# Layer 1: the product with B in front of the last scan, the second gate projection in a done scan's bank, activation bursts in groups 2, 4 and 6; layer 0: three sums instead of four

## The chip, the cores and the metric

The kernel runs on one core of one Trainium2 chip. The metric is device time in microseconds (us). The core's engines work side by side, each with its own queue: TensorE (PE in the profile, PEld for its weight loads), VectorE (DVE), ScalarE (ACT), GpSimd (POOL) and SyncE (SP), which issues DMA transfers here.

## The reference, cut to what matters

The input is (2, 64, 256, 256) in float32. Four layers each add their result to it: x = x + layer(group_norm(x)). Layers 0 and 1 are touched by the change.

```python
# layer 0: nine shifted neighbours, each weighted by a score
feature_score = einsum('bckhw,bchw->bkhw', unfold(em), em)
comp_score = sigmoid(einsum('bckhw,c->bkhw', unfold(inp), w_comp))
out = einsum('bckhw,bkhw->bchw', unfold(inp), comp_score * feature_score)

# layer 1: two Mamba blocks, a layer norm behind each
u, res = split(x @ in_w.T)
u = silu(causal_conv(u) + conv_b)
delta = softplus((u @ xproj_w.T)[..., :r] @ dt_w.T + dt_b)
h = exp(delta * A) * h + delta * B * u        # a scan over all positions, 16 states
y = einsum('bdn,bn->bd', h, C) + u * D
y = layernorm((y * silu(res)) @ out_w.T)
```

## The kernel before

The two batches with 64 channels each fill the 128 partitions; an image row pair, or 512 positions, is the usual tile (128x512). In both layers the order of every engine's queue is the order of the program (`manual_schedule`): an instruction that waits holds up all behind it on its engine.

**Layer 0** goes through 128 steps of two rows. A step t computes the scores of step n = t - 3 on TensorE (`pf`, one matmul for the pixel itself and one for each of four neighbours A, B, C, D), multiplies with the gated features on VectorE (`mult` for the neighbour, `move` for the mirrored neighbour, which another pixel takes up), and adds the terms of step t - 4 with four identity matmuls into `acc` (lines 403 to 411). GpSimd adds the moved products into the terms C, D and B beforehand (lines 400, 401), VectorE those of A.

**Layer 1** cuts the 65536 positions into 128 chunks of 512 for each of two Mambas: 256 tasks that alternate between the first (m = 0) and the second (m = 1, three chunks behind). A task has eight groups, numbered 0 to 7: two batches b of four groups j each; a group has four scans k = 0 to 3. (g,k) below is scan k of group g. A group runs so:

- A product h = delta u B. For j = 2 GpSimd makes it ahead (`product`, line 752; it stands behind group j = 3 of the half before). For the others VectorE makes it (line 773), from B spread over the partitions by a matmul into `pb` (`spread`, line 744, one PSUM bank).
- Four scans on VectorE (line 792), each with its decay `da` from ScalarE (line 789, three PSUM banks in the pool `p_a`).
- On GpSimd the last states are copied (795) and h is multiplied with C (796).
- TensorE sums h over the states into `py` (`before`, line 802), one group later, at the fourth scan.

`gate` (line 652) multiplies a finished `py` with SiLU of the other projection, on VectorE.

Beside the scans, the task that comes two later is prepared by `front` (line 580), a generator that is moved on step by step: load and pad `xin` (`padded`, line 565, copies three columns on GpSimd; for m = 0 only, as the second Mamba's `xin` is written by the norm of the first), convolution of four taps in two halves, the projection for the gate, SiLU, the matmuls for delta and B and C, softplus, and the spill of `bc`, `delta` and `du` to DRAM. `fetch` (line 634) brings these back, laid out for the scans, in groups 1 and 5 of the task before they are used. `layer_norm` (line 656) finishes the task before, in the same way. `aside` (line 691) says in which group each step comes, always at the group's fourth scan. All matmuls of `front` and `layer_norm` take turns in three PSUM banks (`p_mm`). SiLU, softplus and logarithm need other function tables of ScalarE than the decay's exponential, so each makes a burst with a table load at both ends.

Of the kernel before, what the change touches and what calls it, by code (L numbers as in the profile page):

```python
# [10 lines left out]
F32 = mybir.dt.float32  # L11
BF16 = mybir.dt.bfloat16
AF = mybir.ActivationFunctionType
ALU = mybir.AluOpType
# [3 lines left out]
P = 128  # L18
C = 64
# [101 lines left out]
class Kernel:  # L121
# [115 lines left out]
    def layer0(self, x, y, coeffs):  # L237
# [12 lines left out]
        with ExitStack() as ctx:  # L250
# [135 lines left out]
            with tc.manual_schedule(engines={E.PE, E.DVE, E.Activation, E.Pool, E.SP}):  # L386
                features(0)
                for t in range(nstep + 5):
                    if t and t % per == 0:
                        load(t // per + 1)  # L390
                    gated = embed(t) if t < nstep else None
                    if t + 1 < nstep:
                        features(t + 1)

                    n, last = t - 3, t - 4
                    acc = None
                    if 0 <= last < nstep:
                        acc = p_o.tile([P, 2, W], F32, name="acc")
                        if last:
                            for name in "CDB":  # L400
                                add(nc.gpsimd, last, name, moved_to(last, name))

                    def out(name):
                        if acc is not None:
                            nc.tensor.matmul(
                                acc,
                                self.ident,
                                term.pop((last, name)),
                                start=name == "A",
                                stop=name == "B",  # L410
                            )

                    if 0 <= t - 2 < nstep:
                        products(t - 2)
                    if gated:
                        gated()
                    if 0 <= n < nstep:
                        g, _, j = at(n)
                        own = g[:, j : j + 2, inner]
                        pf = score(sq.pop(n))  # L420
                        part = p_s.tile([P, 2, W], F32, name="part")
                        nc.vector.tensor_tensor(part, own, pf, ALU.mult)
                        for i, name in enumerate("ABCD"):
                            pf = score(pr.pop((n, name)))
                            out("ACDB"[i])
                            mult(n, name, near(g, j, name), pf)
                            if name == "A" or n + 1 < nstep:
                                move(n, name, own, pf)
                            if name == "A":
                                nc.vector.tensor_add(part, term[n, name], part)  # L430
                                nc.vector.tensor_add(term[n, name], moved_to(n, name), part)
                    else:
                        for name in "ACDB":
                            out(name)
                    if acc is not None:
                        k, s = divmod(last, per)
                        yt = pool.tile([P, 2, W], F32, name="yt")
                        nc.vector.tensor_add(yt, xt[k][:, 2 * s : 2 * s + 2], acc)
                        nc.vector.bn_stats(stats[:, last, :], yt.rearrange("p r w -> p (r w)"))
                        nc.sync.dma_start(yv[:, 2 * last : 2 * last + 2], yt)  # L440
# [86 lines left out]
    def layer1(self, x, y, coeffs):  # L527
# [4 lines left out]
        with ExitStack() as ctx:  # L532
# [47 lines left out]
            def front(m, i, t):  # L580
# [14 lines left out]
                pr = [p_mm.tile([P, T], F32, name="mm")]  # L595
                mm(pr[0], w["res"][halves[0]], xin[halves[0], 3 : 3 + T])
                yield
                u = pool.tile([P, 2, T], F32, name="u", bufs=3)
                t["u"], t["res"] = u, []
                for b in range(2):  # L600
                    nc.scalar.activation(u[:, b], pv[b], AF.Silu, bias=w["conv_b"])
                pr.append(p_mm.tile([P, T], F32, name="mm"))
                mm(pr[1], w["res"][halves[1]], xin[halves[1], 3 : 3 + T])
                for b in range(2):
                    r = pool.tile([P, T], F32, name="res", bufs=8)
                    nc.scalar.activation(r, pr[b], AF.Silu)
# [9 lines left out]
                delta = pool.tile([P, 2, T], F32, name="delta", bufs=1)  # L616
                for b in range(2):
                    self.softplus(delta[:, b], pd[b], w["dt_b"])
                bc = pool.tile([64, T], F32, name="bc", bufs=3)
                nc.scalar.copy(bc, pb)  # L620
                du = pool.tile([P, 2, T], F32, name="du", bufs=1)
                nc.gpsimd.tensor_tensor(du, delta, u, ALU.mult)
                t["bc"] = bc

                d_bc = spill.tile([2, 32, T], F32, name="d_bc")
                nc.sync.dma_start(d_bc.rearrange("b n t -> (b n) t"), bc)
                d_dl = spill.tile([2, P, T], F32, name="d_dl")
                nc.sync.dma_start(d_dl.rearrange("b c t -> c b t"), delta)
                d_dv = spill.tile([2, P, T], F32, name="d_dv")
                nc.sync.dma_start(d_dv.rearrange("b c t -> c b t"), du)  # L630
                t["spilt"] = d_bc, d_dl, d_dv
# [24 lines left out]
            def layer_norm(m, i, t):  # L656

                po = p_mm.tile([P, T], F32, name="mm")
                for b in range(2):
                    mm(po[C * b : C * b + C], ws[m]["out"], t["res"][b])  # L660
                sq = pool.tile([P, T], F32, name="lsq", bufs=1)
                nc.scalar.activation(sq, po, AF.Square)
                if m == 1:
# [22 lines left out]
            tasks = [(m, i - 3 * m) for i in range(nch + 3) for m in range(2)]  # L686
            tasks = [(m, i) for m, i in tasks if 0 <= i < nch]
            ts = [{} for _ in tasks]
            norm = iter(())

            def aside(n):

                nonlocal norm
                t = ts[n]
                ahead = front(*tasks[n + 2], ts[n + 2]) if n + 2 < len(tasks) else iter(())

                def d(b):
                    t["py"] = p_y.tile([P, T], F32, name="py")
                    mm(t["py"], ws[tasks[n][0]]["d"], t["u"][:, b], True, False)

                def more(b):
                    if n + 1 < len(tasks):
                        fetch(ts[n + 1], b)

                next(norm, None)
                next(ahead, None)
                yield
                d(0)
                next(norm, None)
                more(0)  # L710
                next(ahead, None)
                yield
                next(ahead, None)
                yield
                next(ahead, None)
                yield
                next(ahead, None)
                yield
                d(1)
                more(1)  # L720
                next(ahead, None)
                yield
                if n:
                    norm = layer_norm(*tasks[n - 1], ts[n - 1])
                next(norm, None)
                yield
                next(norm, None)
                yield

            load(0)  # L730
            for n in range(2):
# [3 lines left out]
            with tc.manual_schedule(engines={E.PE, E.DVE, E.Activation, E.Pool, E.SP}):  # L735
# [24 lines left out]
                    )  # L760
                    return h

                ahead = {2: product(*groups[2])}
                pb, before = spread(), None
                for g, (n, b, j) in enumerate(groups):
                    if b == j == 0:
                        steps = aside(n)
                    if j == 0:
                        st = states.tile([P, 4, 4], F32, name=f"st{tasks[n][0]}{b}")
                    t, m = ts[n], tasks[n][0]  # L770
                    if j != 2:
                        h = pool.tile([P, 4, T], F32, name="h", bufs=5)
                        nc.vector.tensor_tensor(  # L773
                            h, t["dv", b], pb.unsqueeze(1).to_broadcast([P, 4, T]), ALU.mult
                        )
                        pb = spread()
                    else:
                        h = ahead.pop(g)
                    if b == j == 0:
                        next(norm, None)  # L780
                    if j == 1 and g > 1:
                        gate(ts[n - 1 + b], 1 - b)
                    for k in range(4):
                        if k == 3:
                            next(steps)
                            if before:
                                before()
                        da = p_a.tile([P, T], F32, name="da")
                        nc.scalar.activation(  # L789
                            da, t["dl", b][:, k], AF.Exp, scale=ws[m]["a"][:, k, j : j + 1]  # L790
                        )
                        nc.vector.tensor_tensor_scan(  # L792
                            h[:, k], da, h[:, k], state[m, b][:, j, k : k + 1], ALU.mult, ALU.add
                        )
# [4 lines left out]
                    if g + 3 < len(groups) and j == 3:  # L799
                        ahead[g + 3] = product(*groups[g + 3])  # L800

                    def before(t=t, h=h, j=j):
                        for k in range(4):
                            mm(t["py"][32 * k : 32 * k + 32], quad, h[:, k], False, j == 3)

                    if j == 3:
                        state[m, b] = st
                before()
                gate(ts[-1], 1)
                for _ in norm:  # L810
                    pass
                for _ in layer_norm(*tasks[-1], ts[-1]):
                    pass
        return self.group_norm("l2", stats, HW // T)


# [523 lines left out]
```

## Time and profile before

| | us |
|---|---|
| median of 3 runs (19418.89 to 19421.33) | 19420.38 |
| profiled execution | 19425.37 |
| its span, first to last instruction | 19423.1 |
| layer 0, step to step | 9.83 |
| layer 1, first to last product with B | 1534.0 to 15693.9 |
| VectorE, TensorE, ScalarE, GpSimd busy | 17991.3, 14534.9, 12151.6, 16845.3 |

Layer 1 is nearly three quarters of the time. A row of the groups of instructions has line, engine, operation, what is written and read with the shapes, how often; then busy time, mean ns of one; then how long the engine was idle just before them, and what ended that. The granted TensorE clock is given as a share of full speed; its mean is 0.756. Two DVE operations that follow each other overlap a little, so starts are closer together than the durations say.

### The profile page before, as it was taken

Reading aid. Unit: us, or ns where it says so; the run is one execution under the profiler, and the core shown is the slowest. Engines: PE = TensorE matmul, PEld = TensorE weight load, DVE = VectorE, ACT = ScalarE, POOL = GpSimd, SP = SyncE. Lnnn points to the kernel's source line nnn. Section 1 sums busy time; section 2 is a strip of 40 time slices with the busy share of each in tenths; the row PEclk is TensorE's granted clock in tenths of the full one; section 3 lists DMA queues with packets and bytes.
Section 4 is the critical chain, followed back from the end, with each engine's and each line's share of the span. In section 5 each row is a group of like instructions: output and inputs, shape, how many; then the busy total and the mean of one; then the engine's idle time right before and its main releaser. Section 6 shows DMA issues by size and latency. Waiting matters only on the chain. (4 is left out here: it accounts for less than half of the span.)

```text
span 19423.1 us, 164029 instructions
## 1 busy us (share of the span) xinstructions
PE 14534.9 (75%) x48720; PEld 4763.2 (25%) x48720; DVE 17991.3 (93%) x15870; ACT 12151.6 (63%) x17418; POOL 16845.3 (87%) x8646
## 2 busy tenths in 40 slices
PE   7996677767777677676677677767777679999996
PEld 3441111111111111111111111111111134444444
DVE  6888999999999999999999999999999978888896
ACT  2325666666666666666666666666666657777774
POOL 5997888888888888888888888888888878888885
PEclk9996666666666666667666666666666679999997
DMA  3116666666666666666666666666666621111104
GB/s 122 57 50 150 149 156 152 150 155 149 155 150 151 156 151 152 150 150 155 152 151 154 149 156 150 150 156 151 152 150 151 154 52 32 32 32 31 32 29 147
DMA packets 662191, 2438.92 MB, mean 126 GB/s; under 512 B 131888, under 2 KB 201264, under 8 KB 450160
## 3 DMA queue, kind: packets, MB, share of 16 engines
q1 hardware_dynamic: 661296, 2428.43, 52.1%
q8 instruction: 385, 6.31, 0.1%
q14 instruction: 510, 4.18, 0.1%
HBM read 1990.14 MB, written 437.78 MB: 125 GB/s over the span
## 5 line engine op out<-in xcount | busy, mean ns | idle before, releaser
L792 DVE TENSOR_TENSOR_SCAN h<-da,st,h 128x512 f32<-128x512 f32 x8192 | 9837.9, 1262 | 310.0 <-ACT da L789 225.5
L796 POOL TENSOR_TENSOR h<-h,cb 128x2048 f32<-128x2048 f32 x2048 | 9252.4, 4518 | 164.7 <-POOL st L795 0.2
L789 ACT ACTIVATE da<-dl,p_a 128x512 f32<-128x512 f32 x8192 | 5564.3, 688 | 3976.2 <-DVE h L792 3884.3
L561 PE MATMUL py<-h,t_c_quad 128*32 128x512 f32 x16384 | 3250.7, 817 | 1649.2 <-POOL h L796 1648.3
L561 PE MATMUL pb<-bc,t_c_sel 64*128 64x512 f32 x3072 | 2696.1, 972 | 2386.6 <-DVE h L773 2381.3
L773 DVE TENSOR_TENSOR h<-dv,pb 128x2048 f32<-128x2048 f32 x1536 | 3471.5, 2260 | 40.8 <-DMA dv<-d_dv 40.8
L1023 POOL TENSOR_TENSOR gl<-gl,prod 128x512 f32<-128x512 f32 x2056 | 2606.1, 1272 | 460.9 <-ACT prod L1019 346.7
L755 POOL TENSOR_TENSOR h<-dv,cb 128x2048 f32<-128x2048 f32 x512 | 2318.7, 4529 | 16.7 <-DMA dl<-d_dl 16.7
L982 DVE SCALAR_TENSOR_TENSOR acc<-z,tap_b,acc 128x1024 f32<-128x1024 f32 (+1 forms) x1496 | 1901.6, 1271 | 22.3
L561 PEld LDWEIGHTS pb<-bc,t_c_sel 64*128 64x128 f32 x3072 | 660.9, 267 | 4410.5 <-DVE h L773 4347.0
L1019 ACT ACTIVATE prod<-z,tap_a 128x512 f32<-128x512 f32 x2056 | 1422.3, 716 | 284.8 <-POOL gl L1023 273.8
L795 POOL COPY st<-h 128x4 f32<-128x4 f32 x2048 | 383.5, 187 | 1362.9 <-DVE h L792 1331.9
L1079 PE MATMUL pcv<-z,diag 128*128 128x512 f32 x2322 | 1236.4, 642 | 179.9 <-ACT gl L1087 166.0
L561 PEld LDWEIGHTS py<-h,t_c_quad 128*32 128x32 f32 x16384 | 423.2, 122 | 3814.4 <-POOL h L796 3222.6
L561 PE MATMUL mm<-xin,p_conv 64*128 64x512 f32 x4096 | 1318.7, 773 | 15.1 <-DMA x1t<-y 15.1
L943 PE MATMUL pz<-t_c_inv,gf 128*128 128x128 f32 (+1 forms) x8192 | 964.7, 293 | 7.6 <-ACT z L951 7.3
L561 PE MATMUL mm<-u,p_dt 128*128 128x512 f32 x1024 | 929.1, 1061 | 0.0
L943 PEld LDWEIGHTS pz<-t_c_inv,gf 128*128 128x128 f32 (+1 forms) x8192 | 792.8, 170 | 484.2 <-issue 302.5
L924 DVE TENSOR_TENSOR gf<-feff,f 128x384 f32<-128x384 f32 x1024 | 558.7, 547 | 299.9 <-PE f L915 297.4
L561 PE MATMUL py<-u,p_d 128*128 128x512 f32 x1024 | 820.9, 895 | 0.0
L951 ACT COPY z<-pz 128x512 f32<-128x512 f32 x768 | 449.7, 590 | 411.1 <-PE pz L943 330.4
L561 PEld LDWEIGHTS mm<-xin,p_conv 64*128 64x128 f32 x4096 | 459.5, 244 | 980.8 <-issue 980.6
(169 smaller groups left out, 17244.8 us busy)
## 6 DMA issues: line engine op xcount, KB each, us to landing
cb<-d_bc SPq DMA_DIRECT2D x2048, 320.0 KB
dl<-d_dl SPq DMA_DIRECT2D x2048, 256.0 KB
dv<-d_dv SPq DMA_DIRECT2D x2048, 256.0 KB
d_dl<-delta SPq DMA_DIRECT2D x256, 512.0 KB
d_dv<-du SPq DMA_DIRECT2D x256, 512.0 KB
xin<-in_x SPq DMA_DIRECT2D x16, 2048.0 KB
xt<-in_x SPq DMA_DIRECT2D x32, 1024.0 KB
y<-yt SPq DMA_DIRECT2D x128, 256.0 KB
```

Source lines behind the costliest of these rows:

```text
L561: nc.tensor.matmul(out, lhsT, rhs, start=start, stop=stop)
L755: nc.gpsimd.tensor_tensor(h, t["dv", b], t["cb", b][:, 0].unsqueeze(1).to_broadcast([P, 4, T]), ALU.mult,)
L773: nc.vector.tensor_tensor(h, t["dv", b], pb.unsqueeze(1).to_broadcast([P, 4, T]), ALU.mult)
L789: nc.scalar.activation(da, t["dl", b][:, k], AF.Exp, scale=ws[m]["a"][:, k, j : j + 1])
L792: nc.vector.tensor_tensor_scan(h[:, k], da, h[:, k], state[m, b][:, j, k : k + 1], ALU.mult, ALU.add)
L796: nc.gpsimd.tensor_tensor(h, h, t["cb", b][:, 1 + j].unsqueeze(1).to_broadcast([P, 4, T]), ALU.mult)
L924: nc.vector.tensor_tensor(o, feff, ph[b], ALU.mult)
L943: nc.tensor.matmul(pz[i * n : (i + 1) * n, k, :, 16 * g : 16 * g + 16], gf[t, 2 * e + g, b][:, c0 : c0 + n], inv, start=True, stop=True,)
L982: eng.scalar_tensor_tensor(out, near(s, name, m0, r, k), w, box["t"], ALU.mult, ALU.add)
L1019: nc.scalar.activation(prod, near(s, name, 4 * h + m, n, k), AF.Copy, scale=w)
L1023: nc.gpsimd.tensor_add(acc, acc, prod)
L1079: nc.tensor.matmul(box["t"], diag[:, k], near(s, f"a{i}", 4 * h + m, n, k), start=k == 0, stop=k == 8,)
```

## The change

In layer 1:

- VectorE's product for a group is made before the fourth scan of the group ahead of it (`direct_product`), instead of at the group's own start.
- Sums of a group into `py` are issued two groups later instead of one. The gates move from the start of groups 1 and 5 to the third scan of groups 2 and 6.
- The steps of `front` and `layer_norm` get places by group and scan (`FRONT`, `NORM`) and are cut finer: the padding of `xin` and the convolution's first half in group 0, the second half in group 1, SiLU in group 2, the matmuls for delta in group 3, softplus in group 4, `bc`, `du` and the spills in groups 5 and 6; of the norm, the projection and the square in group 5, the logarithm in group 6, the rest in group 7.
- The second gate projection goes to a bank of `p_a` instead of `p_mm`, and is issued ahead of the SiLU activations.

In layer 0 VectorE adds the term B into `part`, and GpSimd adds B's moved product into the term D, so that three identity matmuls are left of four.

```diff
@@ layer 0
-                            for name in "CDB":
-                                add(nc.gpsimd, last, name, moved_to(last, name))
+                            for name, moved_by in ("C", "C"), ("D", "D"), ("D", "B"):
+                                add(nc.gpsimd, last, name, moved_to(last, moved_by))
...
-                            out("ACDB"[i])
+                            if i:
+                                out("ACD"[i - 1])
...
-                            if name == "A":
+                            if name in "AB":
                                 nc.vector.tensor_add(part, term[n, name], part)
-                                nc.vector.tensor_add(term[n, name], moved_to(n, name), part)
+                            if name == "B":
+                                nc.vector.tensor_add(term[n, "A"], moved_to(n, "A"), part)
+                                term.pop((n, "B"))
@@ layer 1, front
                 yield
+
+                pr.append(p_a.tile([P, T], F32, name="da"))
+                mm(pr[1], w["res"][halves[1]], xin[halves[1], 3 : 3 + T])
                 u = pool.tile([P, 2, T], F32, name="u", bufs=3)
...
-                pr.append(p_mm.tile([P, T], F32, name="mm"))
-                mm(pr[1], w["res"][halves[1]], xin[halves[1], 3 : 3 + T])
...
                     self.softplus(delta[:, b], pd[b], w["dt_b"])
+                yield
                 bc = pool.tile([64, T], F32, name="bc", bufs=3)
...
                 t["bc"] = bc
+                yield
...
                 nc.sync.dma_start(d_dl.rearrange("b c t -> c b t"), delta)
+                yield
                 d_dv = spill.tile([2, P, T], F32, name="d_dv")
@@ layer 1, layer_norm
                     mm(po[C * b : C * b + C], ws[m]["out"], t["res"][b])
+                yield
                 sq = pool.tile([P, T], F32, name="lsq", bufs=1)
@@ layer 1, aside
+            FRONT = {(0, 1), (0, 3), (1, 3), (2, 3), (3, 3), (4, 3), (5, 1), (5, 3), (6, 0)}
+            NORM = {(5, 0), (5, 2), (6, 3), (7, 1), (7, 3)}
...
+                def at(g, k):
+                    if (g, k) == (2, 1) and n > 1:
+                        next(ts[n - 1].pop("norm"), None)
+                    if n and (g, k) in NORM:
+                        next(t["norm"])
+                    if (g, k) in FRONT:
+                        next(ahead, None)
+                    if g in (2, 6) and k == 3:
+                        d(g // 4)
+                    if g in (1, 5) and k == 3 and n + 1 < len(tasks):
+                        fetch(ts[n + 1], g // 4)
@@ layer 1, the loop over groups
+                def direct_product(n, b, j):
+                    nonlocal pb
+                    h = pool.tile([P, 4, T], F32, name="h", bufs=5)
+                    nc.vector.tensor_tensor(
+                        h, ts[n]["dv", b], pb.unsqueeze(1).to_broadcast([P, 4, T]), ALU.mult
+                    )
+                    pb = spread()
+                    return h
...
-                    if j == 1 and g > 1:
-                        gate(ts[n - 1 + b], 1 - b)
+                    h = ahead.pop(g)
                     for k in range(4):
-                        if k == 3:
-                            next(steps)
-                            if before:
-                                before()
+                        if j == k == 2 and g > 2:
+                            gate(ts[n - 1 + b], 1 - b)
+                        beside(4 * b + j, k)
+                        if k == 3 and len(sums) > 1:
+                            sums.pop(0)()
                         da = p_a.tile([P, T], F32, name="da")
...
+                        if k == 3 and g + 1 < len(groups) and j != 1:
+                            ahead[g + 1] = direct_product(*groups[g + 1])
                         nc.vector.tensor_tensor_scan(
```

More of the change, by code (lines that the diff above doesn't have):

```diff
@@ L409, in out @@
                                 start=name == "A",
-                                stop=name == "B",
+                                stop=name == "D",
                             )
@@ L428, in layer0 @@
                                 move(n, name, own, pf)
-                            if name == "A":
+                            if name in "AB":
                                 nc.vector.tensor_add(part, term[n, name], part)
-                                nc.vector.tensor_add(term[n, name], moved_to(n, name), part)
+                            if name == "B":
+                                nc.vector.tensor_add(term[n, "A"], moved_to(n, "A"), part)
+                                term.pop((n, "B"))
                     else:
-                        for name in "ACDB":
+                        for name in "ACD":
                             out(name)
@@ L688, in layer1 @@
             ts = [{} for _ in tasks]
-            norm = iter(())
+            FRONT = {(0, 1), (0, 3), (1, 3), (2, 3), (3, 3), (4, 3), (5, 1), (5, 3), (6, 0)}
+            NORM = {(5, 0), (5, 2), (6, 3), (7, 1), (7, 3)}
             def aside(n):
-                nonlocal norm
                 t = ts[n]
                 ahead = front(*tasks[n + 2], ts[n + 2]) if n + 2 < len(tasks) else iter(())
+                if n:
+                    t["norm"] = layer_norm(*tasks[n - 1], ts[n - 1])
                 def d(b):
@@ L699, in d @@
                     mm(t["py"], ws[tasks[n][0]]["d"], t["u"][:, b], True, False)
[L701 to L728, printed above, removed]
+                def at(g, k):
[9 more added lines that the diff above has]
+                        fetch(ts[n + 1], g // 4)
+                return at
             load(0)
@@ L761, in product @@
                     return h
-                ahead = {2: product(*groups[2])}
-                pb, before = spread(), None
+                def direct_product(n, b, j):
[6 more added lines that the diff above has]
+                    return h
+                pb, sums = spread(), []
+                ahead = {2: product(*groups[2]), 0: direct_product(*groups[0])}
                 for g, (n, b, j) in enumerate(groups):
                     if b == j == 0:
-                        steps = aside(n)
+                        beside = aside(n)
                     if j == 0:
@@ L770, in layer1 @@
                     t, m = ts[n], tasks[n][0]
[L771 to L780, printed above, removed]
-                    if j == 1 and g > 1:
-                        gate(ts[n - 1 + b], 1 - b)
-                    for k in range(4):
-                        if k == 3:
-                            next(steps)
-                            if before:
-                                before()
+                    h = ahead.pop(g)
+                    for k in range(4):
+                        if j == k == 2 and g > 2:
[3 more added lines that the diff above has]
+                            sums.pop(0)()
                         da = p_a.tile([P, T], F32, name="da")
@@ L800, in layer1, with add_up @@
                         ahead[g + 3] = product(*groups[g + 3])
-                    def before(t=t, h=h, j=j):
+                    def add_up(t=t, h=h, j=j):
                         for k in range(4):
                             mm(t["py"][32 * k : 32 * k + 32], quad, h[:, k], False, j == 3)
+                    sums.append(add_up)
                     if j == 3:
                         state[m, b] = st
-                before()
+                for add_up in sums:
+                    add_up()
                 gate(ts[-1], 1)
[L810 to L813, printed above, removed]
+                for left in (ts[-1]["norm"], layer_norm(*tasks[-1], ts[-1])):
+                    for _ in left:
+                        pass
         return self.group_norm("l2", stats, HW // T)
```

## The prediction

> **What bounds the kernel now.** I read the stretches first (busy microseconds of each engine; PEclk is the granted TensorE clock), then the groups of instructions by line, then the order of time inside one task.
>
> ```profile
> core 0: us, PE busy (x) PEld busy (x) DVE busy (x) ACT busy (x) POOL busy (x), PEclk, DMA share, GB/s
> 600.00:800.00 200.00, 200.00 (x449) 81.66 (x449) 168.00 (x267) 59.99 (x112) 185.75 (x163) 1.00 0.15 54
> 8000.00:9000.00 1000.00, 701.25 (x2062) 167.46 (x2062) 964.34 (x750) 657.48 (x895) 892.50 (x372) 0.69 0.65 152
> ```
>
> The first stretch is layer 0: TensorE is busy all the time at full clock, GpSimd 93%, VectorE 84%. The second is layer 1, 14160 of the 19423 us: VectorE is busy 96%, and TensorE's clock is up only part of the time. So layer 0 is TensorE's, layer 1 VectorE's.
>
> ```profile
> L792 DVE TENSOR_TENSOR_SCAN h<-da,st,h 128x512 f32<-128x512 f32 x8192 | 9837.9, 1262 | 310.0 <-ACT da L789 225.5 <-DVE h L773 2.7
> L773 DVE TENSOR_TENSOR h<-dv,pb 128x2048 f32<-128x2048 f32 x1536 | 3471.5, 2260 | 40.8 <-DMA dv<-d_dv 40.8
> L654 DVE TENSOR_TENSOR res<-res,py 128x512 f32<-128x512 f32 x512 | 349.8, 683 | 199.6 <-PE py L561 198.7
> ```
>
> Layer 1's idle time on VectorE sits in two waits: scans for the decay `da` (225.5 us) and the gates for `py` (198.7 us). Now the order of time; start, length, engine, line.
>
> ```profile
> 8006.65 2.26 DVE L773 TENSOR_TENSOR h<-dv,pb 128x2048 f32<-128x2048 f32 x1
> 8006.80 0.19 POOL L795 COPY st<-h 128x4 f32<-128x4 f32 x1 [1.55 <-DVE h L792]
> 8007.06 4.52 POOL L796 TENSOR_TENSOR h<-h,cb 128x2048 f32<-128x2048 f32 x1
> 8008.83 0.68 DVE L673 TENSOR_TENSOR lsq<-lsq,mm 128x512 f32<-128x512 f32 x1
> 8009.43 4.80 DVE L792 TENSOR_TENSOR_SCAN h<-da,st,h 128x512 f32<-128x512 f32 x4
> 8011.55 4.52 POOL L755 TENSOR_TENSOR h<-dv,cb 128x2048 f32<-128x2048 f32 x1
> 8014.15 2.26 DVE L773 TENSOR_TENSOR h<-dv,pb 128x2048 f32<-128x2048 f32 x1
> 8016.02 0.30 POOL L571 COPY xin<-xin 128x3 f32<-128x3 f32 x2
> 8016.33 0.68 DVE L654 TENSOR_TENSOR res<-res,py 128x512 f32<-128x512 f32 x1
> ```
>
> This is a task's start. On VectorE, starts follow each other by 2.18 us behind a product, 1.18 behind a scan (4.72 for four), 0.60 behind a small product. GpSimd, after a task's last scan, does the state copy, the product with C, the product for group 2, and only then the three-column copy that pads the next `xin`: 9.2 us later.
>
> ```profile
> 8016.46 2.07 PE L561 MATMUL pb<-bc,t_c_sel 64*128 64x512 f32 x2 [2.89 <-DVE h L773]
> 8020.46 3.79 PE L561 MATMUL mm<-xin,p_conv 64*128 64x512 f32 x8
> 8024.18 1.25 PE L561 MATMUL py<-h,t_c_quad 128*32 128x512 f32 x8
> 8025.36 1.99 PE L561 MATMUL mm<-xin,p_conv 64*128 64x512 f32 x8
> 8028.13 1.06 PE L561 MATMUL py<-h,t_c_quad 128*32 128x512 f32 x8
> 8036.52 2.07 PE L561 MATMUL pb<-bc,t_c_sel 64*128 64x512 f32 x2 [4.07 <-DVE h L773]
> 8041.98 0.62 PE L561 MATMUL mm<-u,p_bc 128*32 128x512 f32 x2
> 8050.24 1.89 PE L561 MATMUL mm<-res,p_out 128*64 128x512 f32 x4
> ```
>
> The same half convolution takes 3.72 us (to the next start) after a pause and 1.82 later. The rate doubles 7.7 us into the run that starts at 8016.46, and 5.5 us into that of 8036.52.
>
> ```profile
> 8052.23 0.60 ACT L662 ACTIVATE lsq<-mm 128x512 f32<-128x512 f32 x1 [2.13 <-PE mm L561]
> 8052.73 2.73 ACT L789 ACTIVATE da<-dl,p_a 128x512 f32<-128x512 f32 x4
> ```
>
> ScalarE stands 2.13 us behind the projection for the norm's square, with the next `da` queued behind it; the scan is 0.6 us late for it (8053.45).
>
> **What the Trainium skill says.** "TensorE: Matmul & The Clock Gate", part 1, "What's actually happening": the array runs at half rate by default and goes to full rate after a busy window of about 3.4 us, falling back after an idle one. The trace agrees on the factor (3.72 against 1.82) and is slower on the onset (5.5 and 7.7 us). The same page, "Architectural detail", calls the queues of ScalarE and VectorE strict FIFO; the 2.13 us above, with `da` behind it, agree. "VectorE: DVE Perf Modes", "The DRAIN you can't avoid": an operation that isn't held starts before the last has drained; here a scan that needs the product before it starts 2.36 us after it (8034.20 to 8036.56), an independent operation 2.18.
>
> **The change part by part.** Layer 1 first, per task (8 groups, 256 tasks). The first product starts at 1534.0 and the last, seven eighths into the last task, at 15693.9: 14159.9 / 255.9 = 55.34 us a task. VectorE's own work: 32 scans at 1.18 = 37.76, 6 products at 2.18 = 13.08, two gates and the norm product at 0.60 = 1.80, bn_stats every other task 0.30; together 52.94. So 2.40 are lost: 0.88 and 0.78 by the two rows, 3 products a task followed by a dependent scan at 0.18 = 0.54, and 0.2 of signalling at these places.
>
> *Products in front of the last scan:* no scan follows its own product any more: -0.54. They also give ScalarE 2.18 us in each group that holds a burst. SiLU burst, (2,2) being group 2's third scan: `da` of (2,2) 0.7, table 1.28, two and two activations 2.5, table 1.28, `da` 0.7 = 6.5 from the end of group 1; the last scan of group 2 is due after two scans, gate, scan, product = 6.3, in every other task 0.6 later. Softplus in group 4: 5.3 against 5.7. Logarithm in group 6: 5.3 against 6.3. (A table load has 1283 ns in its row, the activations 0.63 to 0.68.) Those waits go, and at most 0.2 stays in every other task: 0.05 in the sum below.
>
> *Gates at group 2 and 6, sums one group later:* sum of group 7 now stands in group 1, on TensorE behind both halves of the convolution. Count from the start of group 0's first scan. Group 0 with its product takes 6.90, group 1 4.72, two scans 2.36: the gate is due at 13.98. In tasks of the first Mamba (every other one) the convolution needs the padded `xin`, whose copy stays behind GpSimd's product with C and product for group 2, which can't start before the task does: 9.55 by the rows above, 9.65 on TensorE. TensorE's order from there, at the slow rate: half convolution 3.72, sum of group 6 1.85, spread 2.0, half convolution 3.72, gate projection 2.0, sum of group 7 1.85 = 15.1. TensorE has paused 8 us before, so it starts slow. With the rate doubling after 6.6 (mean of the two runs above): 6.6 + 8.5 / 2 = 10.9, so 20.5, and the gate is 6.6 late. Bounds: doubling at 4 us gives 5.3 late, at 10 us 8.3. In tasks of the second Mamba `xin` is long there: TensorE starts at -1.05, and its 17 us, halved after 6.6, end at 10.8: no wait. Per task +3.3 (2.65 to 4.15). Behind the gate SiLU's burst runs on ScalarE while VectorE stands: free.
>
> *Norm moved to group 5:* its projection now follows the spread behind group 5's product, and its square stands before `da` of (5,2). From the start of group 4: product at 3.54, spread 2.31 later, +2.0, projection and signal +2.0, square +0.5, `da` and signal +0.72 = 11.06; the scan is due at 6.90 + 2.36 = 9.26: 1.8 late at the slow rate, on time at the full one. TensorE pauses 3 to 5 us before that (group 2's sum is done by 0 to 3 of this count, the spread starts at 5.85), so slow nearly always: +1.7 (0.9 to 1.85). The old place cost 0.6 in the task shown.
>
> *Gate projection in `p_a`, fronts and DMAs moved:* the second projection waits for scan (2,0), done at 12.9. TensorE comes to it at 20.5, behind the late gate's sum, or at 10.8 in the other tasks, where SiLU's burst starts only at 13.7; without that cover it would cost the 2.0 of one slow projection. On SP the spills of `bc` and `delta` now stand ahead of group 5's fetch and that of `du` behind it; softplus is over in group 4, so they don't hold the fetch up, and what is fetched is used 40 us later. GpSimd gets no new work: 49.4 us a task, its product for group 2 ends at 9.4, due at 11.62; for group 6, 2.4 early.
>
> Sum: 52.94 + 3.3 + 1.7 + 0.05 = 57.99 against 55.34: +2.65, times 256 = +678 us.
>
> *Layer 0, 128 steps of 9.83 us* (two starts of `yt`: 800.47, 810.30). One identity matmul less: 0.86, TensorE 8.97. One more add on VectorE, 0.73 where the next needs it: 8.21 of starts without waits to 8.94. GpSimd keeps three adds: 185.75 of 200 us = 9.13 a step, now the longest; two adds in a row on one tile may add 0.1. New step 9.13 to 9.4, taken 9.22: -78 us (-55 to -90).
>
> 19423 + 678 - 78 = 20023 in the profiled execution's span. That execution took 19425.4, its median is 19420.4: 20020.
>
> **Rivals.** *Gate alone:* TensorE is still fast at the norm's projection, and the square costs nothing. For it: the sum just before. Against: a pause of 2.41 us before 8048.40 was enough for the rate to fall (the sum there takes 1.84, not 1.0). 52.94 + 3.35 = 56.29: +0.95 x 256 - 78 = 19590. *TensorE never speeds up in the run:* gate 10.8 late, 5.4 a task, with 1.85: +4.85 x 256 - 78 = 20590. Against: both runs above sped up within 8 us. *Faster:* TensorE is at full rate from the convolution's start on and at the norm. Then the gate comes at 9.65 + 7.55 = 17.2, 3.2 late, 1.6 a task; the square is free: 52.94 + 1.65 = 54.6, -0.74 x 256 - 78 = 19155. It decides where the waits on VectorE come to less than 2.40 + 0.30 (layer 0's 78 us) = 2.7 a task. For it: 0.69 mean clock shows much fast running; against: an 8 us pause before. *The change does nothing that shows:* gains and waits cancel, 19420.
>
> **How the numbers follow.** Forecast 0.66, gate alone 0.15, never fast 0.09, faster 0.08, cancel 0.02. The forecast's own range is the bounds of the two waits and layer 0: 52.94 + 2.65 + 0.9 to 52.94 + 4.15 + 1.85 + 0.2, that is +1.15 and +3.8: 19630 to 20340. With the gate-alone case and a margin for waits not seen: 19560 to 20400; never fast, faster and cancel lie outside. About 0.2% is what a measurement of this kernel can tell from no change. Faster 0.08, within 0.02, slower 0.90.
>
> **What would show it.** Right: VectorE's gate line with some 800 us idle by `py`, in every other task near 6 us each; `xin`'s copy named as what TensorE waits for; scans waiting for `da` by some 400 us, all at group 5's third; the step of layer 0 near 9.2 with GpSimd full. Wrong: gates without waits in tasks of the first Mamba, or a task under 55.6 us.

## The result and the profile after

The changed kernel takes 19867.8 us (median of 4 runs, 19864.19 to 19868.83), the kernel before 19419.6 (median of 4): a ratio of 1.0231, with a 95% interval of 1.0213 to 1.0248. The profiled execution spans 19866.0 us, 443 more than before.

The busy time of each engine in the two stretches, as for the kernel before:

```profile
core 0: us, PE busy (x) PEld busy (x) DVE busy (x) ACT busy (x) POOL busy (x), PEclk, DMA share, GB/s
600.00:800.00 200.00, 200.00 (x437) 77.12 (x436) 190.35 (x306) 62.99 (x117) 198.36 (x175) 1.00 0.17 59
8000.00:9000.00 1000.00, 661.18 (x1980) 164.65 (x1980) 922.03 (x723) 621.31 (x859) 861.20 (x358) 0.70 0.63 148
```

In layer 1 every engine is busy for less of the time than before, VectorE 922 us of 1000 instead of 964. No engine has become the bound: they wait for each other more. The groups of instructions by line say where VectorE waits:

```profile
L791 DVE TENSOR_TENSOR_SCAN h<-da,st,h 128x512 f32<-128x512 f32 x8192 | 9888.2, 1260 | 447.9 <-ACT da L786 447.7
L764 DVE TENSOR_TENSOR h<-dv,pb 128x2048 f32<-128x2048 f32 x1536 | 3467.0, 2257 | 41.8 <-DMA dv<-d_dv 41.8
L661 DVE TENSOR_TENSOR res<-res,py 128x512 f32<-128x512 f32 x512 | 340.7, 665 | 678.5 <-PE py L564 678.5
```

The scans' wait for `da` has gone from 225.5 to 447.7 us, the gates' wait for `py` from 198.7 to 678.5. The view of waits (who waits for whom: total, how often, the longest) gives the counts:

```profile
PEld mm L564 <- POOL xin L574: 1274.0, 126, 10.1
ACT lsq L670 <- PE mm L564: 722.2, 256, 11.6
DVE res L661 <- PE py L564: 678.5, 126, 7.6
DVE h L791 <- ACT da L786: 447.7, 256, 2.7
```

The gate waits in 126 tasks, so every other one, 5.4 us each; and just as often TensorE waits for the columns that pad `xin`, which it did not in the kernel before. The scans wait once in each of 256 tasks, 1.75 us, in all but one at group 5's third scan. The first product starts at 1453.9 us and the last at 16137.2, so a task takes 14683.3 / 255.9 = 57.38 us, where it took 55.34: +523 us in all. Layer 0 ends 80 us earlier. The two make the 443.

One late gate in order of time (start, length, engine, line); the task's first scan starts at 8059.70, that is 1.18 after the first line:

```profile
8058.52 4.79 DVE L791 TENSOR_TENSOR_SCAN h<-da,st,h 128x512 f32<-128x512 f32 x4
8058.65 2.07 PE L564 MATMUL pb<-bc,t_c_sel 64*128 64x512 f32 x2 [5.07 <-DVE h L764]
8060.12 4.51 POOL L795 TENSOR_TENSOR h<-h,cb 128x2048 f32<-128x2048 f32 x1
8064.60 4.50 POOL L753 TENSOR_TENSOR h<-dv,cb 128x2048 f32<-128x2048 f32 x1
8065.42 8.32 DVE L791 TENSOR_TENSOR_SCAN h<-da,st,h 128x512 f32<-128x512 f32 x7
8069.05 0.18 POOL L574 COPY xin<-xin 128x3 f32<-128x3 f32 x1
8069.28 3.78 PE L564 MATMUL mm<-xin,p_conv 64*128 64x512 f32 x8 [8.56 <-POOL xin L574]
8073.00 1.93 PE L564 MATMUL py<-h,t_c_quad 128*32 128x512 f32 x8
8077.62 1.02 PE L564 MATMUL mm<-xin,p_res 64*128 64x512 f32 x2
8078.57 1.06 PE L564 MATMUL py<-h,t_c_quad 128*32 128x512 f32 x8
8079.70 0.69 DVE L661 TENSOR_TENSOR res<-res,py 128x512 f32<-128x512 f32 x1 [5.96 <-PE py L564]
```

A copy of three columns, 0.18 us long, stands behind two GpSimd products of 4.5 us. TensorE starts 9.58 us after the task's first scan, at the slow rate, and the gate's sum (8078.57) stands behind all of this work in its queue. The scans end about 8073.7, and VectorE stands for 6 us. In the kernel before the copy has the same place behind GpSimd's products (8016.02), but its convolution comes a group later (8020.46) and finds it done. The wait of group 5's third scan:

```profile
8037.12 2.07 PE L564 MATMUL pb<-bc,t_c_sel 64*128 64x512 f32 x2 [4.78 <-DVE h L764]
8039.12 1.97 PE L564 MATMUL mm<-res,p_out 128*64 128x512 f32 x4
8041.14 0.60 ACT L670 ACTIVATE lsq<-mm 128x512 f32<-128x512 f32 x1 [2.76 <-PE mm L564]
8041.63 2.73 ACT L786 ACTIVATE da<-dl,p_a 128x512 f32<-128x512 f32 x4
8042.35 4.81 DVE L791 TENSOR_TENSOR_SCAN h<-da,st,h 128x512 f32<-128x512 f32 x4 [1.74 <-ACT da L786]
```

ScalarE has the norm's square ahead of the decay, and the square needs a projection that TensorE makes at the slow rate behind a spread.

### The profile page after: what moved, and what is told of

Its sections match the earlier page's. It is cut to its first block, busy times and chain, and to the rows that moved or that the text cites. A ratio compares the mean times of both kernels' runs of the same rounds, so it can differ in the third digit from the quotient of the medians.

```text
span 19866.0 us, 161606 instructions
## 1 busy us (share of the span) xinstructions
PE 14236.8 (72%) x48464; PEld 4739.0 (24%) x48464; DVE 17966.0 (90%) x15998; ACT 12031.5 (61%) x17418; POOL 16840.5 (85%) x8646
## 4 chain that ended last, share of the span: by engine, by line
DVE 33%; PE 19%; DMA 19%; POOL 9%; ACT 9%; issue 9%; SPq 2%; POOLq 0%; DVEq 0%; ACTq 0%
DVE h L791 17%; DVE h L764 9%; DMA cb<-d_bc 7%; DMA dl<-d_dl 6%; PE mm L564 4%; POOL h L753 3%; POOL gl L1023 3%; DVE acc L982 3%; PE pf L361 3%; DMA dv<-d_dv 2%; PE pcv L1079 2%; PE acc L405 2%; ACT da L786 2%; PE py L564 2%; POOL h L795 2%
## 5 line engine op out<-in xcount | busy, mean ns | idle before, releaser
L791 DVE TENSOR_TENSOR_SCAN h<-da,st,h 128x512 f32<-128x512 f32 x8192 | 9888.2, 1260 | 447.9 <-ACT da L786 447.7
L786 ACT ACTIVATE da<-dl,p_a 128x512 f32<-128x512 f32 x8192 | 5484.4, 685 | 3905.6 <-DVE h L791 3858.3
L564 PE MATMUL pb<-bc,t_c_sel 64*128 64x512 f32 x3072 | 2447.0, 887 | 2824.0 <-DVE h L764 2824.0
L564 PE MATMUL py<-h,t_c_quad 128*32 128x512 f32 x16384 | 3178.2, 807 | 9.4 <-POOL h L795 9.4
L564 PE MATMUL mm<-xin,p_conv 64*128 64x512 f32 x4096 | 1847.3, 832 | 1091.6 <-POOL xin L574 1075.8
L564 PE MATMUL py<-u,p_d 128*128 128x512 f32 x1024 | 874.3, 950 | 654.2 <-DVE res L661 654.2
L564 PEld LDWEIGHTS mm<-xin,p_conv 64*128 64x128 f32 x4096 | 710.1, 256 | 1894.1 <-POOL xin L574 1274.0
L661 DVE TENSOR_TENSOR res<-res,py 128x512 f32<-128x512 f32 x512 | 340.7, 665 | 678.5 <-PE py L564 678.5
```

The costliest lines, as they stand in the source:

```text
L564: nc.tensor.matmul(out, lhsT, rhs, start=start, stop=stop)
L786: nc.scalar.activation(da, t["dl", b][:, k], AF.Exp, scale=ws[m]["a"][:, k, j : j + 1])
L791: nc.vector.tensor_tensor_scan(h[:, k], da, h[:, k], state[m, b][:, j, k : k + 1], ALU.mult, ALU.add)
```

## The experiments

Ratios are against the kernel before, gains in us against the changed kernel's median. Beside the experiments the kernel before took 19422 to 19426 us, against 19419.6 beside the changed kernel, so a gain is known to some 6 us. The lines of code are of the changed kernel unless it says otherwise.

**Padding on ScalarE** (`e1_pad`), which takes away what the convolution waits for:

```diff
-nc.gpsimd.tensor_copy(t[:, 0:3], last[m][:, T : T + 3])
+nc.scalar.copy(t[:, 0:3], last[m][:, T : T + 3])
```

> The changed kernel with the three-column copy that pads xin on ScalarE instead of GpSimd, so that it no longer stands behind GpSimd's product with C and product for group 2. Theory (the first gate of every other task waits 5.3 us for a convolution that waits for this copy): both kinds of task lose this wait, 128 x 5.27 = 675 us less than the changed kernel, 19190 us, faster than before; VectorE's idle time at the gate near 0. Rival (the gate is late because its sum is issued behind the convolution, whatever starts that): the wait stays in both kinds of task, 19870 us.

Measured: 19194.7 us, ratio 0.9882 (0.9868 to 0.9897), 673 less. The groups by line:

```profile
L791 DVE TENSOR_TENSOR_SCAN h<-da,st,h 128x512 f32<-128x512 f32 x8192 | 9909.5, 1268 | 446.8 <-ACT da L786 444.9
L661 DVE TENSOR_TENSOR res<-res,py 128x512 f32<-128x512 f32 x512 | 340.4, 665 | 7.6 <-PE py L564 7.6
```

The gates' 678.5 us are down to 7.6, the scans' wait is as it was, and the time fell by what the gates lost. With the copy out of GpSimd's queue the whole gate wait is gone.

**The norm's square half a group later** (`e2_square`), ahead of a first scan's decay instead of a third's, so that the projection has two scans, 2.36 us, more:

```diff
-NORM = {(5, 0), (5, 2), (6, 3), (7, 1), (7, 3)}
+NORM = {(5, 0), (6, 0), (6, 3), (7, 1), (7, 3)}
```

> The changed kernel with the norm's square moved from (5,2) to (6,0), behind all decays of group 5. Theory (the third scan of group 5 is 1.8 us late in every task, because its decay is queued on ScalarE behind a square that waits for TensorE): 256 x 1.81 = 463 us less than the changed kernel, 19405 us, about the time before. Rival (the wait only moves, to the first scan of group 6 or to the logarithm's burst): 19650 to 19870 us, with the idle time before scans unchanged in sum.

Measured: 19462.0 us, ratio 1.002 (1.0012 to 1.0028), 406 less. The scans' row:

```profile
L791 DVE TENSOR_TENSOR_SCAN h<-da,st,h 128x512 f32<-128x512 f32 x8192 | 9896.3, 1271 | 36.9 <-POOL h L753 33.7 <-ACT da L786 1.7
```

The scans' 447.7 us behind `da` are 1.7: all of that wait was the square's place. 463 were expected; the wait was smaller than that to begin with, and 33.7 us of waits for GpSimd's product and 16 more at the gates (694.2 us) are new.

**Both edits** (`e3_both`).

> The changed kernel with both: xin's pad copied on ScalarE and the norm's square at (6,0). Theory (the two waits are the whole loss and add up): 19868 - 675 - 463 = 18730 us, 3.5% faster than before, a task of 53.0 us with VectorE busy all the time in layer 1. Rival (one wait covers the other, or GpSimd, 49.4 us of work a task, takes over as the bound): 18900 to 19200 us with new waits for GpSimd's products.

Measured: 18775.6 us (18770.80 to 18780.77), ratio 0.9668 (0.9652 to 0.9684), 1092 less than the changed kernel; 673 and 406 add to 1079, and 1138 were expected. This version is faster than both kernels. Its stretch of layer 1, and the scans' row:

```profile
8000.00:9000.00 1000.00, 691.05 (x2153) 178.85 (x2152) 998.22 (x783) 674.92 (x949) 927.39 (x368) 0.76 0.68 159
L791 DVE TENSOR_TENSOR_SCAN h<-da,st,h 128x512 f32<-128x512 f32 x8192 | 9895.9, 1270 | 40.4 <-POOL h L753 36.4 <-ACT da L786 0.6
```

VectorE is busy 99.8% of the time. From its first product to its last, 1450.3 to 15036.2, a task takes 53.09 us: the 52.94 of VectorE's own work and 0.16 of waits (40.4 us in the scans' row over 256 tasks). Of the scans' waits for `da`, 0.6 us are left: no activation burst is late any more.

**Extra matmuls in TensorE's pause, of 64 rows** (`e4_warm`): five spreads, written to a bank that the convolution then overwrites, ahead of it for every chunk of the first Mamba, to raise TensorE's rate before the convolution comes. `warm` is an older task's `bc`. The output doesn't change.

```diff
+if m == 0 and "warm" in t:
+    for _ in range(5):
+        mm(pv[0], sel[:, 0, 0], t["warm"])
```

> The changed kernel with five spread matmuls more (their result is overwritten, no output changes) on TensorE ahead of the convolution's first half in tasks that prepare the first Mamba, where TensorE pauses for xin's pad. Theory (about 7.6 of the 11 us between that copy and the late gate are work at full rate, the rest is the slow TensorE clock after the pause): the gate's wait falls from 5.3 to about 3 us, 19580 us. Rival (the clock has no part; the convolution only gets more in front of it): the wait is 5.3 us or more, 19870 us or above.

Measured: 19863.6 us, ratio 1.0228 (1.0213 to 1.0243): no change, and the gates wait 675.1 us. **The same with matmuls of 128 rows** (`e7_warm128`), `warm` being an older task's `u`:

```diff
-        mm(pv[0], sel[:, 0, 0], t["warm"])
+        mm(pv[0], self.ident, t["warm"][:, 0])
```

> As e4_warm, but the five matmuls ahead of the convolution read 128 rows (the identity times u) instead of 64. In e4_warm the run of 64-row matmuls from 8054.6 on did not raise the TensorE clock before 8068, after the convolution had started; 64 rows may not count as busy. Theory (the slow clock is part of the gate's 5.3 us): with 128 rows the clock is up when the convolution starts, the gate's wait falls to about 3 us, 19580 us. Rival (whatever runs before, the convolution starts slow or the clock has no part): 19860 us again.

Measured: 19613.6 us, ratio 1.0096 (1.0079 to 1.0113), 254 less; the gates wait 427.0 us. TensorE in order of time with 64 rows:

```profile
8054.61 2.07 PE L564 MATMUL pb<-bc,t_c_sel 64*128 64x512 f32 x2 [5.09 <-DVE h L769]
8056.47 8.74 PE L564 MATMUL mm<-bc,t_c_sel 64*128 64x512 f32 x10
8065.24 3.39 PE L564 MATMUL mm<-xin,p_conv 64*128 64x512 f32 x8
```

And with 128 rows:

```profile
8052.37 2.07 PE L564 MATMUL pb<-bc,t_c_sel 64*128 64x512 f32 x2 [5.08 <-DVE h L769]
8054.37 6.81 PE L564 MATMUL mm<-u,t_c_ident 128*128 128x512 f32 x10
8063.01 1.99 PE L564 MATMUL mm<-xin,p_conv 64*128 64x512 f32 x8 [1.82 <-POOL xin L574]
```

The granted clock (third figure from the end) in the stretch of 64-row matmuls, then with 128 rows before and after it rises:

```profile
8054.61:8065.24 10.63, 10.60 (x13) 3.83 (x13) 10.63 (x9) 4.36 (x7) 9.35 (x5) 0.50 1.05 233
8052.12:8058.93 6.81, 6.56 (x8) 2.47 (x9) 6.81 (x6) 2.77 (x4) 5.28 (x3) 0.50 1.07 240
8058.95:8063.01 4.06, 2.24 (x7) 0.69 (x5) 4.06 (x5) 1.60 (x3) 4.06 (x3) 1.00 1.02 229
```

With 64 rows the clock is at half through 10.6 us of matmuls without a pause (ten take 8.7 us), and the convolution still starts slowly (3.32 us to the next start). Ten of 128 rows take 6.8, as the clock rises to full among them, and the convolution behind them takes 1.92 to the next start. It is the same in the other tasks: of 125 late gates, the clock stood at half at the start of every convolution with 64 rows, and at full at every one with 128. So the first test never pulled its lever and says nothing of what a higher rate is worth; the second does. At full rate the gate still waits 427.0 / 126 = 3.4 us, of which the convolution's start at 9.58 and 7.55 of work at full rate explain 3.15 (17.13, due at 13.98). So with the copy as late as it is, 251 of the 678.5 us are the slow rate behind it; the other 427 stay at full rate, and only `e1_pad` takes them away. Here more work for TensorE made the kernel faster.

**Layer 0 alone** (`e5_layer0`): the kernel before with the changed layer 0, whose diff stands above.

> The kernel before with the change's layer 0 alone (three identity matmuls instead of four, B added on VectorE and GpSimd). Theory (the step goes from 9.83 to 9.19 us because TensorE was the bound, and GpSimd's 9.15 us become it): 128 x 0.64 = 82 us less than before, 19338 us. Rival (VectorE's additional add costs as much as TensorE gains): 19420 us.

Measured: 19346.4 us, ratio 0.9959 (0.9947 to 0.9972), 79 less than the kernel before, near the 82 expected. A step takes 9.21 us (`yt` at 803.63 and 812.84).

**The product alone** (`e6_product`): the kernel before, with VectorE's product made before the last scan of the group ahead, and all else in its old place.

```diff
+ahead = {2: product(*groups[2]), 0: direct_product(*groups[0])}
...
+h = ahead.pop(g)
...
+if k == 3 and g + 1 < len(groups) and j != 1:
+    ahead[g + 1] = direct_product(*groups[g + 1])
```

> The kernel before with one part of the layer 1 change alone: VectorE's product with B is made in front of the last scan of the group ahead of it. Gates, sums, front, norm and layer 0 stay as before. Theory (three products a task no longer hold up the scan that needs them, 0.18 us each, and the 2.18 us cover the SiLU burst's 0.74 and the square's 0.27 us): 256 x 1.55 = 397 us less than before, 19023 us. Rival (the product only takes the place of the waits, because the sums or the decays it pushes back are late next): 19280 us, the 138 us of the dependent scans alone, or 19420.

Measured: 19608.6 us, ratio 1.0094 (1.0079 to 1.0110): slower, and neither the theory nor the rival said so. The rows of the scans and of the products:

```profile
L796 DVE TENSOR_TENSOR_SCAN h<-da,st,h 128x512 f32<-128x512 f32 x8192 | 9895.7, 1262 | 640.9 <-ACT da L791 640.8
L766 DVE TENSOR_TENSOR h<-dv,pb 128x2048 f32<-128x2048 f32 x1536 | 3473.7, 2262 | 131.8 <-PE pb L561 91.0 <-DMA dv<-d_dv 40.8
```

Two bursts in order of time, on ScalarE and VectorE:

```profile
8006.62 1.27 ACT L601 ACTIVATE u<-mm,t_p_conv_b 128x512 f32<-128x512 f32 x2
8008.03 2.26 DVE L766 TENSOR_TENSOR h<-dv,pb 128x2048 f32<-128x2048 f32 x1
8010.44 2.73 ACT L791 ACTIVATE da<-dl,p_a 128x512 f32<-128x512 f32 x4
8011.16 4.81 DVE L796 TENSOR_TENSOR_SCAN h<-da,st,h 128x512 f32<-128x512 f32 x4 [0.87 <-ACT da L791]
8019.84 3.62 DVE L796 TENSOR_TENSOR_SCAN h<-da,st,h 128x512 f32<-128x512 f32 x3
8021.38 1.27 ACT L525 ACTIVATE delta<-mm,t_p_dt_b 128x512 f32<-128x512 f32 x2
8025.14 4.81 DVE L796 TENSOR_TENSOR_SCAN h<-da,st,h 128x512 f32<-128x512 f32 x4 [1.68 <-ACT da L791]
```

`da` has three banks, so ScalarE is at most three scans ahead, and a burst is covered only by what VectorE does in those three. The old places put softplus ahead of group 5's last decay, and as group 6's product is GpSimd's, no product of VectorE stands in front of that scan: it comes 1.68 us late. This place alone has 400 us of waits, in 254 tasks, where the kernel before had none; nearly all the rest is the SiLU burst (the first of the two), which was late before too: 167 us then, 237 now. The same product does cover the bursts in `e3_both`, where they stand in groups 2, 4 and 6, each with a product of VectorE ahead of its last scan. The balance: 415 us more behind `da`, 91 behind the spread that the product reads, 172 less at the gates (27.0 us are left) and, by the forecast's 0.18 each, 138 less for scans behind their own product. That is 196 more, and 183 were measured against the 19425.5 us of the kernel before in the same set. The move of the product and the bursts' places belong together; the first without the second costs 0.9%.

**The second gate projection back in `p_mm`** (`e8_p_mm`), in `e3_both`:

```diff
-pr.append(p_a.tile([P, T], F32, name="da"))
-mm(pr[1], w["res"][halves[1]], xin[halves[1], 3 : 3 + T])
 u = pool.tile([P, 2, T], F32, name="u", bufs=3)
...
+pr.append(p_mm.tile([P, T], F32, name="mm"))
+mm(pr[1], w["res"][halves[1]], xin[halves[1], 3 : 3 + T])
```

> The kernel of e3_both with the second gate projection back in the pool p_mm and behind the SiLU activations, as before the change. Theory (the projection then waits for the first SiLU to free its bank and stretches the burst in group 2 past the scan that needs its decay): 0.5 to 1 us a task later, 18900 to 19030 us, with idle time before scans for da. Rival (the burst has room enough, or another wait covers it): 18776 us, no difference.

Measured: 18954.8 us, ratio 0.9758 (0.9743 to 0.9772), 179 more than `e3_both`. The scans' row of the groups:

```profile
L791 DVE TENSOR_TENSOR_SCAN h<-da,st,h 128x512 f32<-128x512 f32 x8192 | 9875.3, 1261 | 217.5 <-ACT da L786 175.7 <-POOL h L753 39.3
```

The burst in order of time:

```profile
8036.29 1.48 PE L564 MATMUL mm<-xin,p_res 64*128 64x512 f32 x2 [2.54 <-ACT u L605]
8037.80 0.60 ACT L610 ACTIVATE res<-mm 128x512 f32<-128x512 f32 x1 [0.50 <-PE mm L564]
```

`p_mm` has three banks, which hold the two convolutions and the first projection, so the second needs the bank that SiLU reads and can only stand behind it: bank and place in the queue are one edit. ScalarE stands half a microsecond inside its burst, and 175.7 us of waits for `da` come back, all at group 2's last scan. The other bank is worth 0.7 us a task in this version; no run tried it in the changed kernel.

**The sums ahead of the fronts' steps in each half's first two groups** (`e9_sum_first`), so that the gate's sum doesn't stand behind the convolution:

```diff
+first = k == 3 and j < 2 and len(sums) > 1
+if first:
+    sums.pop(0)()
 beside(4 * b + j, k)
-if k == 3 and len(sums) > 1:
+if k == 3 and not first and len(sums) > 1:
```

> The changed kernel with the sums of groups 0, 1, 4 and 5 issued on TensorE ahead of the front's and norm's steps instead of behind them; xin's pad stays behind GpSimd's products. Theory (the gate's wait is made of all that stands on TensorE between the pad and the sum of group 7): one sum and one half convolution with the gate projection move behind the gate's sum, which leaves 3.7 + 2.0 + 1.9 us at the slow rate behind the pad at 9.6, so 17 instead of 19.3: 128 x 2.2 = 280 us less than the changed kernel, 19590 us. Rival (only the copy counts): no difference, 19868 us.

Measured: 19582.7 us, ratio 1.0081 (1.0066 to 1.0096), 285 less. Two rows of the groups:

```profile
L794 DVE TENSOR_TENSOR_SCAN h<-da,st,h 128x512 f32<-128x512 f32 x8192 | 9891.8, 1261 | 709.5 <-ACT da L789 709.3
L661 DVE TENSOR_TENSOR res<-res,py 128x512 f32<-128x512 f32 x512 | 340.9, 666 | 121.6 <-PE py L564 121.6
```

The gates wait 557 us less, the scans 262 more: 295 net, near the 285. What is late next is the SiLU burst, which needs the same late convolution, and holds `da` up behind it: 2.1 us each at group 2's last scan, in 126 tasks. That the theory's 280 came so near was luck: it expected a gate still 3 us late (it is 1.0) and no wait at the scans. So the queue's order alone is half a cure; TensorE waits for `xin` in 126 tasks here too (1062.6 us before weight loads), and both waits stand behind that.

## Why the prediction came out as it did

- **The late gate: right in place and cause.** Counted from the task's first scan: the padding's copy was put at 9.55 us and is at 9.35; the convolution 9.65 against 9.58; the gate due 13.98 and 13.98. It waits in every other task, and `e1_pad` shows the copy behind it.
- **Its size was the term that was off.** "With the rate doubling after 6.6 (mean of the two runs above)" gave a gate 6.6 us late, 3.3 a task. Measured: 5.4, and 678.5 / 256 = 2.65. The trace's record of the granted clock shows why. It rises to full 2.9 to 6.0 us after the late convolution's start, 4.5 on the mean of 125 tasks (5.8 in the one shown): 9.58 + 7.55 + 4.5 / 2 = 19.38, which is 5.4 late. In the forecast's two runs it rises at 8024.60 and 8041.67, so 8.1 and 5.2 us after their starts; the 7.7 and 5.5 were read from durations and have the same mean. But both runs begin with a spread, a matmul of 64 rows, and the late convolution doesn't: it comes behind a pause, of 8.6 us in the task shown. `e4_warm` shows that such matmuls didn't raise the rate, even in 10.6 us. Over all runs like the first (256) the mean is 6.5 from the spread and 4.5 from the 128-row matmul behind it; over those like the second (254) it is 5.9 and 3.9. So 6.6 was no odd sample: it was counted from a matmul too early. The error of 0.65 a task, times 256, is 166 us; the span came 157 below the sum's 20023.
- **The square:** 1.7 a task forecast, 1.75 measured, at group 5's third scan, as forecast; `e2_square` shows the cause. The rival in which it costs nothing fell.
- **The products and the bursts:** no scan follows its own product now, and with the two late waits gone nothing of the bursts is left (`e3_both`). The 52.94 us of VectorE's own work, the base of the sum, are what that version runs at.
- **The gate projection in `p_a`** was costed at nothing, and the changed kernel has no wait of VectorE there. `e8_p_mm` shows that in the version with both repairs the bank gains 179 us; whether it gains anything in the changed kernel stays open.
- **Layer 0:** 9.22 a step forecast, 9.19 in the changed kernel (`yt` at 805.49 and 814.68), 80 us in all where 78 were forecast; GpSimd is its longest engine, 198.36 us of 200, as forecast. The two adds on one tile in a row:

```profile
800.29 1.28 POOL L381 TENSOR_TENSOR term<-term,mvD 128x512 f32<-128x512 f32 x1
801.65 1.27 POOL L381 TENSOR_TENSOR term<-term,mvB 128x512 f32<-128x512 f32 x1
```

They start 1.36 us apart, against 1.22 for two adds on separate tiles in the kernel before (800.10 and 801.32): 0.14, where the forecast allowed 0.1.

- **The rivals:** "never speeds up" falls by the sum at 8078.57, which takes 1.06 us; "faster" would have needed the full rate at the convolution's start and at the norm. The first alone isn't enough: `e7_warm128` has it and is 0.96% slower than the kernel before, since the square's wait stays (445.1 us); its gates wait 427.0 / 256 = 1.67 a task, where that rival had 1.6. "Gate alone" falls by the square's 1.75 a task.

With the two repairs the schedule is worth 2.25 us a task (55.34 to 53.09), 576 us. Two of its placements hid that: the convolution and the gate's sum behind it came to depend on a small copy that stood behind long work in another queue, and the norm's square stood two scans too early.

## What to carry to other kernels

When a step moves, ask what stands ahead of its smallest instruction on that instruction's engine: 0.18 us of copy behind 9 us of products cost 673 us, and moving it to an engine with slack took one line. A burst on an engine that runs ahead by a fixed number of buffers is covered only by the other engine's long work inside that number, so move both or neither. And where a change loses, take away the new waits one by one before undoing it: the gain may lie beneath them.

## What the hardware showed that was not expected

- **Matmuls of 64 rows did not raise TensorE's rate** in 10.6 us without a pause, where the clock rose 4.6 us after the first 128-row one. The Trainium skill, "TensorE: Matmul & The Clock Gate", part 1, "What's actually happening", speaks of time, not of a number of matmuls: a window of about 3.4 us in which the engine is busy, and which runs freely. For this kernel's single 64-row matmuls the 10.6 us don't agree, and the measurement decides. The convolution's matmuls also have 64 rows, but come in pairs for the two batches, and they do raise the rate: behind 42 of the 125 late starts it rose after about 2.9 us, while nothing else had run since the pause. What is counted, rows in use or something else, wasn't separated; the two tests differ in weights and data too.
- **The onset varies because the clock changes on a grid.** All 1402 records of the granted clock in the changed kernel's trace begin within 0.03 us of a multiple of 3.413 us, counted from the first, which agrees with that window. So the same convolution finds the full rate after 2.9 us in one task and after 6.0 in another, as its start falls in the grid. One or two tasks are too few to read a mean onset from.
